# A decoder layer with 64 experts: more expert weights loaded ahead, fewer shared pieces between the experts, wider steps in the last norm

## The chip, the cores and the metric

The kernel runs on one core of a Trainium2 chip. A core has five engines with an instruction queue each: TensorE (PE, matrix products), VectorE (DVE), ScalarE (ACT), GpSimd (POOL) and SyncE (SP, which here only issues transfers). Each works through its own queue in order and waits on semaphores for the others. PE writes to PSUM, from which DVE or ACT must copy a result before its buffer can be written again; all else lies in SBUF or in DRAM. The metric is the device time of one execution in microseconds, lower is better; one number stands for the median of several runs.

## The reference, cut to what matters

The input `x` is 32 batches of 256 tokens of width 256, 8192 tokens in all, in float32. Three sub-layers follow each other, each with a residual and a layer norm after it:

```python
x = _layernorm(x + _L0_attn_ref(x, ...))
x = _layernorm(x + _L0_xattn_ref(x, ctx_1024, ctx_1024, ...))
x = _layernorm(x + _L0_ffn_ref(x, ...))
```

The first two are self-attention with rotary embedding and a differential cross-attention, 16 heads each. The third is a mixture of 64 experts: a router picks 6 experts for each token; each expert takes at most 96 tokens, and computes `gelu(xs @ w1) @ w2` with a hidden width of 128; a token's six results are added with its routing weights. Beside them a shared network of hidden width 512 works on every token:

```python
y = jnp.einsum('ecf,efh->ech', hmid, w2).reshape(E * CAP, h)
out = jnp.zeros((t, h), x.dtype).at[token_of].add(y_pair)
shared = jax.nn.gelu(x @ sw1.T, approximate=True) @ sw2.T
return (out + shared).reshape(b, s, h)
```

## The kernel before, in words

There are two stages, each an `ExitStack` of pools. In the **first stage** (lines 322 to 1141) the 32 batches pass through both attentions. Its end stores, for each batch, the normalised tokens in transposed form in DRAM (`x2T_d`), starts the first accumulator `acc[0]` with them and the second, `acc[1]`, with zeros (`store`, line 1092), and scatters each token's row to the slots of its six experts (`dispatch`, line 1076, POOL's indirect DMAs into `slots`). Small POOL copies (`fence`, line 427) read a `pt` tile in between.

The **shared network** is a generator, `shared` (line 242), over 16 blocks of 512 tokens (`NBLK`). One `next` does one piece: half of a block's first product (8 matmul instructions, into a `two` bank of PSUM, tile `two`), or half of the second product of the block before (16 instructions, into tile `one`). A block is four pieces, 64 in all. The evacuation of a piece on ACT (a GELU into `gT`, or a copy into the block's result `ys[k]`) is kept in `unread` and issued at the next piece by `settle` (line 237). Every fourth piece also issues a load of `x2T` three blocks ahead on SP. Sixteen pieces are issued in the first stage, 48 are left for the second. The results of blocks 0 to 2 have buffers of their own, those of blocks 3 to 15 come from `ypool`.

The **second stage** (lines 1144 to 1367) is a loop over slots. Wrappers named `InOrder` (line 163) hold each engine to the order in which the program issues its instructions. The 64 experts make 32 pairs, `NP`; a pair n passes through four slots from slot n + START on: `turn` (four PE transposes of its rows `xs` into PSUM, copied by DVE to `xsT`), `up` (eight products with `w1`, GELU on ACT to `hT`), `down` (four products with `w2`), and `scatter` (line 1235), in which DVE multiplies by the routing weights into `ye` and POOL issues two indirect DMAs that add the 96 rows of each expert to `acc[0]` and `acc[1]`. The scatter of a pair to one accumulator must wait until that of the pair before has landed. There are six `ye` buffers, eight `xs` buffers, and in PSUM four `one` and two `two` tiles.

The weights of a pair are one tile of 512 KB from the `four` pool, which has ten buffers used in turn (`next_four`, line 1157). `expert_weights` issues the load on SP, `rows_of` the load of the pair's rows. Weights of the first six pairs are issued in slot 1, rows of the first six in slot START - 2, and from then on the rows and weights of pair n + 6 together, after `down(n)` (`fetch_for`, line 1322). A piece of the shared network is issued in each slot below START, and then in two slots out of three until END = START + 35.

From END on, a slot takes a piece, or two in every fourth slot, and one **step of the last norm** (`Last`, line 1258). Block k passes through five parts: `fetch` (SP loads its two accumulators into two `four` tiles, 512 KB each; the first waits for all scatters), `add` (POOL adds them), `stats` (DVE adds the shared result `ys[k]` and takes mean and variance), `scale` (two small ACT instructions, then `rstd` and `off` on POOL), and `put` (four ACT instructions into a third `four` tile, and the output's DMA from ACT's queue). In one step the parts of different blocks are issued in the order of the tuple in lines 1350 to 1356: `fetch` of block s, `add` of s - 1, `scale` of s - 3, `put` of s - 4, `stats` of s - 2. A step whose `stats` needs a shared result that is not yet issued is put off to the next slot (line 1349), while the pieces go on.

Of the kernel before, what the change touches and what calls it, by code (L numbers as in the profile page):

```python
# [12 lines left out]
F32 = mybir.dt.float32  # L13
# [24 lines left out]
def tile_decoder_layer(  # L38
# [194 lines left out]
    NBLK = NT // TB  # L233
    EARLY = min(3, NBLK)
    ys, whole, unread = {}, set(), []
# [86 lines left out]
    with ExitStack() as one:  # L322
# [8 lines left out]
        AHEAD = min(5, B)  # L331
# [812 lines left out]
    with ExitStack() as two:  # L1144

        four = two.enter_context(tc.tile_pool(name="four", bufs=1))
        psum.append(Apart(two))
        wk = two.enter_context(tc.tile_pool(name="wk2", bufs=2))
        small = two.enter_context(tc.tile_pool(name="small2", bufs=3))
        ypool = two.enter_context(tc.tile_pool(name="ypool", bufs=NBLK - EARLY - 1))  # L1150
        ypools.append(ypool)
        AHEAD = 6
        START = 7

        fours = itertools.count()

        def next_four(shape):

            return four.tile(shape, F32, name=f"four{next(fours) % 10}")

        def rows_of(n):

            xs = wk.tile([CAP, 2, XPW], F32, name=f"xs{n % 8}", bufs=1)
            sp.dma_start(
                out=xs,
                in_=slots[2 * n * CAP : (2 * n + 2) * CAP, :].rearrange("(e s) d -> s e d", s=CAP),
            )
            return xs

        def tokens_of(n):  # L1170

            code = xs_of[n][:, :, D + NE]
            empty = small.tile([CAP, 2], F32, tag="empty", name="empty")
            dve.tensor_scalar(empty, code, 0.0, slot_f[:CAP, :], ALU.is_equal, ALU.mult)
            token = small.tile([CAP, 2], F32, tag="token", name="token")
            dve.tensor_scalar(token, code, -1.0, float(NT), ALU.mult, ALU.add)
            idx = small.tile([CAP, 2], I32, name=f"idx{n % 12}", bufs=1)
            dve.tensor_add(idx, token, empty)
            return idx

        def expert_weights(n):

            wt = next_four([P, 2, D // P * F + D])
            sp.dma_start(out=wt, in_=w12[n])
            return wt
# [72 lines left out]
        class Last:  # L1258
# [4 lines left out]
            def fetch(self):  # L1263
                self.sums = []
                for n in range(2):
                    a = next_four([P, NQ, D])
                    sp.dma_start(
                        out=a, in_=acc[n][self.rows, :].rearrange("(p q) d -> p q d", q=NQ)
                    )
                    self.sums.append(a)  # L1270
# [23 lines left out]
            def put(self):  # L1294
                o = next_four([P, NQ, D])
                for q in range(NQ):
                    act.activation(
                        o[:, q, :],
                        ys[self.k][:, q, :],
                        AF.Identity,  # L1300
                        scale=self.rstd[:, q : q + 1],
                        bias=self.off[:, q : q + 1],
                    )
                act.dma_start(
                    out=flat[self.rows, :].rearrange("(p q) d -> p q d", q=NQ), in_=o
                )

        NP = NE // 2
        pairs = [Pair(n) for n in range(NP)]
        xs_of, idx_of, weights_of = {}, {}, {}  # L1310
        last = [Last(k) for k in range(NBLK)]
        END = START + NP + 3
        slot = steps = 0
        more = True

        def pieces_on(n):
            nonlocal more
            for _ in range(n):
                if more:
                    more = next(pieces, "end") != "end"  # L1320

        def fetch_for(n):
            if n < NP:
                xs_of[n] = rows_of(n)
                weights_of[n] = expert_weights(n)

        while more or steps < NBLK + 5:
            n = slot - START

            if 0 <= n - 1 < NP:  # L1330
                pairs[n - 1].turned()
            if 0 <= n - 2 < NP:
                pairs[n - 2].gelu()
            if 0 <= n - 3 < NP:
                pairs[n - 3].scatter()
            if slot == 1:
                for k in range(AHEAD):
                    weights_of[k] = expert_weights(k)
            if slot == START - 2:
                for k in range(AHEAD):  # L1340
                    xs_of[k] = rows_of(k)
            if 0 <= n < NP:
                idx_of[n] = tokens_of(n)

            if slot < START or slot < END and n % 3 < 2:
                pieces_on(1)
            elif slot >= END:
                pieces_on(1 if slot % 4 else 2)
            if slot >= END and (not 2 <= steps < NBLK + 2 or steps - 2 in whole):
                for part, behind in (  # L1350
                    (Last.fetch, 0),
                    (Last.add, 1),
                    (Last.scale, 3),
                    (Last.put, 4),
                    (Last.stats, 2),
                ):
                    if 0 <= steps - behind < NBLK:
                        part(last[steps - behind])
                steps += 1
            if 0 <= n < NP:  # L1360
                pairs[n].turn()
            if 0 <= n - 1 < NP:
                pairs[n - 1].up()
            if 0 <= n - 2 < NP:
                pairs[n - 2].down()
                fetch_for(n - 2 + AHEAD)
            slot += 1


# [60 lines left out]
```

## Time and profile before

| | us |
|---|---|
| median of 6 runs | 1899.2 (1891.34 to 1909.41) |
| the profiled execution's own time | 1895.92 |
| its span in the profile | 1894.2 |
| first piece of the second stage on PE | 1589.6 |
| first turn of a pair on PE | 1627.46 |
| first and last scatter-add issued by POOL | 1636.06, 1812.49 |
| last product of a pair on PE ends | 1786.2 |
| last product of all on PE ends | 1863.9 |
| last output issued by ACT | 1890.54 |

Over the whole span PE is busy for 1803.0 us (95%), ACT 1057.3, DVE 1247.9 and POOL 1192.1; this is the mean of two very different stages, and says little about the second. All instructions carry line 173, that of the helper `InOrder`, so they are told apart by their tiles: `two<-x2T,w_s` and `one<-w_s,gT` are pieces of the shared network, `one<-ident,xs`, `one<-xsT,four` and `one<-four,hT` the turn, up and down of a pair, `acc<-ye,idx` a scatter-add, `four<-in_w` a load of weights, `xs<-slots` of rows, `four<-acc` a fetch of the last norm, `rs`, `rstd` and `off` its scale, `four<-y,off,rstd` its put.

A row of a timeline gives the start, the duration of the run of instructions, the engine (SPq and ACTq are the queues that issue DMAs), line, operation, output and inputs, the count, and in brackets how long the engine was idle before and what released it. A row of the waits gives who waited for whom, total, times and longest. A row of the windows gives, for each engine, its busy time and the number of instructions, then the granted PE clock (1.00 is full), the mean busy share of the 16 DMA engines and the GB/s that they moved.

### The profile page before, as it was taken

The numbers are of one execution on the slowest core, as the hardware profiler recorded it, in microseconds if no ns is written. First come the engines' busy times: TensorE is split into PE (matmuls) and PEld (weight loads), VectorE is DVE, ScalarE is ACT, GpSimd is POOL, SyncE is SP. The second block draws the span as 40 slices with busy tenths as digits, with TensorE's granted clock in tenths as the row PEclk, the third lists the DMA queues.
The fourth block names the chain that finished last, engine by engine and source line by source line (L and its number), as shares of the span: only waits on it lengthen the run. The fifth ranks groups of instructions, "written<-read, shape, count | busy, mean of one in ns | idle before, by whom it ended". The sixth has DMA issues, their size and how long they took to land. (4 is left out here: it accounts for less than half of the span.)

```text
span 1894.2 us, 44636 instructions
## 1 busy us (share of the span) xinstructions
PE 1803.0 (95%) x17800; PEld 1312.4 (69%) x17800; DVE 1247.9 (66%) x2755; ACT 1057.3 (56%) x1807; POOL 1192.1 (63%) x1366
## 2 busy tenths in 40 slices
PE   6999999999999999999999999999999899897973
PEld 4777777777777777777777777777776566575742
DVE  5566677777777777777777777777777452242246
ACT  1666666666666666666666666666666552322237
POOL 7444445777777666777666776666555577244667
PEclk9999999999999999999999999999999899899987
DMA  3080111211111111111111111111112021786478
GB/s 116 15 185 18 32 32 50 70 49 45 39 36 38 35 34 35 35 37 35 36 34 32 33 32 33 33 34 34 32 29 79 18 85 50 233 227 169 81 236 311
DMA packets 109552, 132.16 MB, mean 70 GB/s; under 512 B 33019, under 2 KB 94676, under 8 KB 109344
## 3 DMA queue, kind: packets, MB, share of 16 engines
q1 hardware_dynamic: 78832, 106.83, 18.6%
q0 software_dynamic: 25600, 13.02, 4.1%
q10 hardware_dynamic: 4912, 9.46, 1.3%
q8 instruction: 140, 2.29, 0.5%
q14 instruction: 68, 0.56, 0.1%
HBM read 74.62 MB, written 111.04 MB: 98 GB/s over the span
## 5 line engine op out<-in xcount | busy, mean ns | idle before, releaser
L173 DVE TENSOR_REDUCE pad_mx<-all 128x4 f32<-128x1024 f32 (+1 forms) x512 | 588.9, 1187 | 230.9 <-PE all L173 226.0
L173 ACT ACTIVATE pt<-all 128x512 f32<-128x512 f32 (+3 forms) x768 | 516.6, 740 | 246.2 <-PE all L173 190.0
L173 PE MATMUL all<-qT,kT 32*128 32x256 f32 (+1 forms) x4096 | 517.4, 389 | 3.9 <-DVE qT L173 2.8
L173 PE MATMUL all<-kT,qT 32*128 32x256 f32 (+1 forms) x4096 | 514.6, 386 | 5.6 <-DVE qkb L173 3.0
L173 POOL DMA_INDIRECT slots<-xpt,slot x384 | 387.2, 1008 | 144.3 <-issue 141.6
L173 PEld LDWEIGHTS all<-qT,kT 32*128 32x128 f32 (+1 forms) x4096 | 359.7, 181 | 134.5 <-issue 83.0
L173 PEld LDWEIGHTS all<-kT,qT 32*128 32x128 f32 x4096 | 363.1, 185 | 17.5 <-DVE qkb L173 3.4
L173 POOL TENSOR_TENSOR qT<-qT,mT 128x512 f32<-128x512 f32 x126 | 160.1, 1292 | 135.1 <-ACT mT L173 135.1
L173 PE MATMUL all<-w_qkv,xT 128*128 128x512 f32 (+1 forms) x512 | 183.1, 492 | 8.5 <-DMA xT<-in_xT 8.5
L173 ACT COPY ot<-all 128x512 f32<-128x512 f32 x192 | 112.1, 589 | 94.1 <-PE all L173 90.1
L173 POOL DMA_INDIRECT acc<-ye,idx x64 | 90.2, 1410 | 114.1 <-DVE ye L173 40.6
L173 POOL COPY fence<-pt 120x1 f32<-120x1 f32 (+1 forms) x154 | 28.7, 188 | 165.1 <-ACT pt L173 165.1
L173 PEld LDWEIGHTS all<-w_qkv,xT 128*128 128x128 f32 x512 | 93.7, 193 | 50.7 <-issue 34.8
L173 PE MATMUL all<-pt,pad_xv 120*32 120x256 f32 x2048 | 117.6, 381 | 2.9 <-ACT pt L173 2.8
L173 ACT COPY T<-all 128x512 f32<-128x512 f32 x128 | 73.1, 591 | 80.8 <-PE all L173 77.7
L173 PE MATMUL all<-pt,pad_v 128*32 128x256 f32 x2048 | 117.1, 381 | 0.0
L173 POOL TENSOR_TENSOR rc<-qkb,cosr 128x512 f32<-128x512 f32 x62 | 78.8, 1272 | 51.1 <-DVE qkb L173 50.6
L173 POOL TENSOR_TENSOR pad_qk<-rc,qkb 128x256 f32<-128x256 f32 x124 | 102.5, 848 | 2.7
L173 PE MATMUL all<-ident,ot 128*128 128x128 f32 x768 | 103.4, 278 | 0.1
L173 PE MATMUL two<-x2T,w_s 128*128 128x512 f32 x176 | 84.1, 628 | 19.1 <-ACT gT L173 19.1
L173 PE MATMUL one<-w_s,gT 128*128 128x256 f32 x416 | 95.2, 385 | 5.7 <-DVE ye L173 3.1
L173 PEld LDWEIGHTS all<-ident,ot 128*128 128x128 f32 x768 | 83.6, 141 | 21.5 <-ACT pt L173 13.5
(156 smaller groups left out, 2917.7 us busy)
## 6 DMA issues: line engine op xcount, KB each, us to landing
four<-in_w SPq DMA_DIRECT2D x32, 512.0 KB, 4.5
four<-acc SPq DMA_DIRECT2D x32, 512.0 KB, 6.9
xT<-in_xT SPq DMA_DIRECT2D x32, 256.0 KB, 3.8
xt<-in_x SPq DMA_DIRECT2D x32, 256.0 KB, 4.1
x2T_d<-T SPq DMA_DIRECT2D x32, 256.0 KB, 2.5
acc<-xpt SPq DMA_DIRECT2D x32, 256.0 KB, 2.7
acc<-zero SPq DMA_DIRECT2D x32, 256.0 KB, 3.4
x2T<-x2T_d SPq DMA_DIRECT2D x16, 512.0 KB, 6.9
```

Source lines behind the costliest of these rows:

```text
L173: ins = f(*args, **kwargs)
```

## The change

The pool `four` gets 14 buffers in place of 10, and `ypool` 8 in place of 12, so the room is the same. The weights of 14 pairs are issued in slot 1, and after `down(n)` the rows of pair n + 6 and the weights of pair n + 14. The first pair starts in slot 6 in place of 7. While pairs pass, a shared piece is issued in one slot of three in place of two. In the last norm `add`, `stats`, `scale` and `put` follow `fetch` by 2, 3, 5 and 6 steps in place of 1, 2, 3 and 4; a step is put off when its `stats`, now three steps behind, lacks its shared result.

```diff
-        ypool = two.enter_context(tc.tile_pool(name="ypool", bufs=NBLK - EARLY - 1))
+        ypool = two.enter_context(tc.tile_pool(name="ypool", bufs=8))
...
         AHEAD = 6
-        START = 7
+        FOURS = 14
+        START = 6
...
-            return four.tile(shape, F32, name=f"four{next(fours) % 10}")
+            return four.tile(shape, F32, name=f"four{next(fours) % FOURS}")
...
-        def fetch_for(n):
-            if n < NP:
-                xs_of[n] = rows_of(n)
-                weights_of[n] = expert_weights(n)
-
-        while more or steps < NBLK + 5:
+        def fetch_after(n):
+
+            if n + AHEAD < NP:
+                xs_of[n + AHEAD] = rows_of(n + AHEAD)
+            if n + FOURS < NP:
+                weights_of[n + FOURS] = expert_weights(n + FOURS)
+
+        while more or steps < NBLK + 7:
...
-                for k in range(AHEAD):
+                for k in range(FOURS):
                     weights_of[k] = expert_weights(k)
...
-            if slot < START or slot < END and n % 3 < 2:
+            if slot < START or slot < END and n % 3 == 0:
                 pieces_on(1)
             elif slot >= END:
                 pieces_on(1 if slot % 4 else 2)
-            if slot >= END and (not 2 <= steps < NBLK + 2 or steps - 2 in whole):
+            if slot >= END and (not 3 <= steps < NBLK + 3 or steps - 3 in whole):
                 for part, behind in (
                     (Last.fetch, 0),
-                    (Last.add, 1),
-                    (Last.scale, 3),
-                    (Last.put, 4),
-                    (Last.stats, 2),
+                    (Last.add, 2),
+                    (Last.scale, 5),
+                    (Last.put, 6),
+                    (Last.stats, 3),
                 ):
...
-                fetch_for(n - 2 + AHEAD)
+                fetch_after(n - 2)
```

## The prediction

> **What bounds the kernel now.** The change touches only the second stage, from 1589.6 us on; everything before it stays as it is. I read the waits first, then the stage in windows, then the engines one by one in the timeline. What TensorE (PE) waited for in this stage:
>
> ```profile
> engine line waited for: us in total, times, longest us
> PE two L173 <- ACT gT L173: 19.1, 2, 12.0
> PE one L173 <- DVE ye L173: 10.7, 5, 3.7
> ```
>
> No weight tile stands among PE's releasers: PE never waited for an expert's weights. It waited twice for a GELU on ScalarE (ACT), 7.1 us at 1610 and 12.0 us at 1817, and for `ye` in between. The timeline of GpSimd (POOL) says why: the scatter-adds into `acc` form two chains, one for each accumulator, in which each waits until the one before has landed.
>
> ```profile
> 1702.30 1.41 POOL L173 DMA_INDIRECT acc<-ye,idx  x1 [4.75 <-DVE ye L173]
> 1704.01 1.41 POOL L173 DMA_INDIRECT acc<-ye,idx  x1 [0.30 <-issue]
> 1708.52 1.41 POOL L173 DMA_INDIRECT acc<-ye,idx  x1 [3.11 <-DVE ye L173]
> ...
> 1798.74 1.41 POOL L173 DMA_INDIRECT acc<-ye,idx  x1 [0.97 <-DMA acc<-ye,idx]
> 1800.45 1.41 POOL L173 DMA_INDIRECT acc<-ye,idx  x1 [0.30 <-issue]
> 1802.85 1.41 POOL L173 DMA_INDIRECT acc<-ye,idx  x1 [0.99 <-DMA acc<-ye,idx]
> ```
>
> A pair takes 6.22 us at 1702 and 4.11 us at 1799. The windows show what differs:
>
> ```profile
> core 0: us, PE busy (x) PEld busy (x) DVE busy (x) ACT busy (x) POOL busy (x), PEclk, DMA share, GB/s
> 1637.86:1760.23 122.37, 111.28 (x589) 84.57 (x588) 41.59 (x141) 26.40 (x40) 53.53 (x39) 0.97 0.77 202
> 1760.23:1812.49 52.26, 52.26 (x226) 36.80 (x226) 10.60 (x35) 14.22 (x16) 33.80 (x24) 1.00 0.45 55
> ```
>
> While SyncE's (SP) queue moves weights and rows (DMA share 0.77), 19 pairs take 122.37 us, 6.44 each; after the last load at 1754 (share 0.45), 12 pairs take 52.26 us, 4.36 each. `ye` has six buffers, so PE runs six pairs ahead and then stands still with the chain. I call S the issue of the last scatter, 1812.5. Everything later hangs on it: the last norm's first fetch waits for the scatters.
>
> **The sum, part by part.** Unit costs from PE's timeline: a shared piece (`two<-x2T,w_s` or `one<-w_s,gT`) takes 3.43 us (two start at 1786.20, the next at 1793.07); turn, up and down of a pair take 2.09 us (1696.21 to 1698.30).
>
> *Weights earlier.* They cannot start earlier than now:
>
> ```profile
> 1605.70 0.20 POOL L173 COPY fence<-pt 120x1 f32<-120x1 f32 x1
> 1605.93 2.81 SPq L173 DMA_DIRECT2D four<-in_w  x6
> ```
>
> SP waited 33.0 us for that POOL instruction. So 14 loads leave at 1605.93 and not 6, ahead of the `x2T` load and of the rows `xs` on the same queue. At the 400 GB/s of the windows 1608 to 1616 one load of 512 KB moves in 1.31 us: 14 x 1.31 = 18.3, `x2T` 1.31, the first rows 0.87 (240.8 KB at 285 GB/s, windows 1616 to 1624), and some 2.2 us until they land (3.1 median less 0.87): 1628.7. The first turn is at 1627.46 now, with one piece after it; with START = 6 that piece goes, but PE comes out of a pause and finds the next rows 0.87 us apart. I take the first scatter 1 us earlier (1635); bounds 3 us earlier, 3 later.
>
> Later each slot issues rows for n+6 as before and weights for n+14. These go into the buffer that `down(n)` has just read, so SP now waits for PE; behind it are the next slot's rows, needed four slots later, and `x2T`, needed twelve pieces later: nothing.
>
> *The scatter chain.* Its excess now is 19 x (6.44 - 4.36) = 39.6 us. SP moved 24 rows (20.9 us), 24 weights (31.4) and 5 `x2T` (6.6) in that time, 58.9 us: 0.67 us of delay for each us of transfer. After: 25 rows (21.8), 18 weights (23.6), 3 `x2T` (3.9), 49.3 us, so 33.0 of excess: **6.6 us gained**. Bounds: nothing gained, if the delay comes with the rows, which stay; 39.6 if it vanished wholly. Proportion is nearest to the rows I have. S becomes 1812.5 - 6.6 - 1 = 1804.9.
>
> *One piece in three slots.* 48 pieces remain at the stage's start, both times. Before, 31 are done by the end of the pairs (7 + 24); after, 18 (6 + 12). PE work per pair falls from 4.4 to 3.2 us, beside a chain of 4.4 to 6.4 us which PE only follows: nothing gained there. But **30 pieces instead of 17, 13 x 3.43 = 44.6 us, move behind the pairs**. Part fills PE's time while the scatters drain. Now the last `down` ends at 1786.2, S - 26.3, and that lead stays.
>
> One rule stands against these emptier slots. After a pause of 2.28 us at 1713 four `down` matmuls took 1.65 us, not 1.03, and the piece after them 4.80, not 3.60. The Trainium skill (TensorE: Matmul & The Clock Gate, What's actually happening) says that PE falls to half rate after an idle window of about 3.4 us. By it a pieceless slot would cost 4.2 us of PE and three slots 15.3, which is 2.2 over three unloaded periods, some 9 us for the last 12 pairs. The sum takes nothing for it. By the row a pause costs 0.6 + 1.2 = 1.8 us of PE; a loaded pair leaves PE 3.2 us idle and an unloaded one 1.1, with six pairs of lead to draw on. Bounds: 0, and 12 x (1.8 - 1.1) = 8.4 us.
>
> *Steps further apart.* ACT works in order, and its `scale(0)` waits for the first fetch, its sum and its statistics. Evacuations behind it wait too, so PE stops when PSUM is full. Now and then:
>
> ```profile
> 1813.75 3.60 PE L173 MATMUL two<-x2T,w_s 128*128 128x512 f32 x8
> 1829.32 6.51 PE L173 MATMUL two<-x2T,w_s 128*128 128x512 f32 x8 [11.98 <-ACT gT L173]
> 1835.67 7.07 PE L173 MATMUL one<-w_s,gT 128*128 128x256 f32 x32
> ```
>
> PE resumes at S + 16.8, and its first piece takes 2.9 us more than usual. After, `scale(0)` stands in the sixth slot of the end. Seven pieces are issued by then, with six evacuations ahead of it on ACT; the next ones fill two `two` and four `one` buffers, so PE does 12 pieces, 41.2 us, up to S + 14.9. The 13th needs a `two` whose GELU stands on ACT behind `put(0)`; that waits for `rstd(0)`, and on POOL `add(3)` comes before it, where `add(2)` did:
>
> ```profile
> 1827.27 3.24 POOL L173 TENSOR_TENSOR four<-four,four 128x1024 f32<-128x1024 f32 x1 [0.23 <-DMA four<-acc]
> 1830.47 1.05 POOL L173 TENSOR_TENSOR rstd<-rs,mhalf 128x4 f32<-128x4 f32 x1
> 1831.59 0.24 POOL L173 TENSOR_TENSOR off<-off,rstd 128x4 f32<-128x4 f32 x1
> ```
>
> Adds started at 1821.15, 1824.70 and 1827.27, so a fourth some 10 us after the first, S + 18.5, ends at S + 20.9; `rstd` and `off` take 1.4 (S + 22.3), `put(0)` 2.08 and its DMA issue 0.38, an evacuation 0.49, the GELU 1.8, handovers 0.6: **PE resumes at S + 27.6**. It has 18 pieces left, 61.7 us, and the slow start of 2.9: PE ends at **S + 92.2** (now S + 51.4).
>
> The steps cost ACT 2.77 us each (0.29 + 2.10 + 0.38, start to start) and POOL 3.63. In a slot, 1.25 pieces cost ACT 1.4 and PE 4.3, so PE leads by little. The fetches, outputs and late `x2T` loads, some 27 MB at 390 GB/s, 69 us from S + 5, end earlier. The 14 buffers let seven blocks come at once; that brings nothing while PE ends last.
>
> *Tail.* Step 18 waits for the last piece. Behind it on ACT: an evacuation 0.49, three `scale` 0.87, four `put` 8.4, three DMA issues 1.14, and 3.7 from the last issue to the span's end (1890.5 to 1894.2): 14.6. End: 1804.9 + 92.2 + 14.6 = **1911.7, 17.5 us longer** than the span of 1894.2. The profiled execution's own time is 1895.9, so 1913.4; the median shown, 1899.2, is 3.3 above that execution, so **1916.7**.
>
> *Smaller `ypool`.* Block 11 reuses block 3's buffer; its writer and the reader that frees it are both on ACT, `put(3)` ahead of it in program order. No wait. It costs only if an evacuation came first; it does not.
>
> **Rivals.** *Weights alone delay the scatters* (for it: they move the most; against: rows go with every one of the 19 slow pairs). Then from pair 11 on, PE being six ahead at weight 17, the chain runs at 4.36: excess 11 x 2.08 = 22.9, 16.7 gained, 10.1 more than forecast: +7.4, **1906.6**. *The chain runs free* and ends on the other side: loads seven pairs further ahead no longer meet the scatters, S = 1812.5 - 39.6 - 1 = 1771.9, end 1878.7, -15.5, **1883.7**. It decides against me from S = 1777.9 (1884.7 - 106.8) down; 18 weights and 25 rows still flowing speak against it. *ACT ends last, or PE is cold*: ACT's 4.2 us a slot against PE's 4.3 leaves no room; half a us more in each of some 18 slots, or the 8.4 us above, adds 9 and gives +26.5, **1925.7**. *The change does nothing* is true of its weights (no wait for them exists); the pieces move all the same, so I give it nothing of its own.
>
> **How the numbers follow.** Forecast 0.62, around 1916.7, with its own range 1909 to 1923; weights alone 0.18; ACT or cold PE 0.13; free chain 0.07. What a measurement of this kernel tells from no change is about 0.5%, 9.5 us. Weights alone falls within it; the forecast's range begins above. Slower 0.75, same 0.18, faster 0.07. The range leaves out the free chain and the ends beyond: 1900 to 1929.
>
> **What would show it.** Right: first weights still near 1606, first rows near 1628; the last scatter near 1805, slow pairs up to about the 12th to 19th; a PE pause of 10 us or more after the last scatter; PE busy until some 15 us before the end, with four `put` behind it. Wrong: S below 1780; PE pausing little after S; PE done 25 us or more before the end, as now.

## The result and the profile after

The changed kernel takes 1912.72 us (median of 20 runs, 1909.95 to 1919.30), the kernel before 1901.26 us (46 runs, 1889.40 to 1912.06): the ratio is **1.0069 [1.0055, 1.0084]**, slower by about 0.7%. (The ratio with its 95% interval is not quite the quotient of the two medians, which is 1.0060.) The profiled execution took 1915.67 us, with a span of 1914.0.

The second stage is read in three parts, for every kernel of this study: the **start**, from the POOL `fence` copy that releases SP (1605.70 before, 1607.82 after) to the first scatter; the **chain**, from the first scatter to the issue of the last, S; and the **end**, from S to the end of the span. Counting from the fence takes out what the first stage does: over all the executions below except two on a chip of their own, the end of the first stage scatters by 6.7 us without a change in its code. These are the windows of the kernel before, cut at these points (columns as in the prediction's windows):

```profile
1605.70:1636.06 30.36, 23.25 (x94) 15.89 (x93) 4.08 (x17) 10.57 (x11) 3.13 (x5) 0.83 0.76 238
1636.06:1812.49 176.43, 165.34 (x821) 122.93 (x821) 52.19 (x175) 40.62 (x56) 88.83 (x63) 0.98 0.67 158
1812.49:1894.20 81.71, 39.22 (x135) 26.16 (x133) 53.03 (x144) 51.15 (x109) 60.25 (x49) 0.76 0.84 311
```

And of the changed kernel:

```profile
1607.82:1641.47 33.65, 20.88 (x75) 14.99 (x74) 3.99 (x17) 8.03 (x9) 3.13 (x5) 0.80 0.84 286
1641.47:1804.23 162.76, 140.49 (x708) 104.89 (x707) 51.96 (x175) 30.97 (x47) 88.78 (x63) 0.94 0.66 144
1804.23:1914.00 109.77, 80.01 (x275) 52.65 (x273) 64.94 (x144) 63.45 (x120) 71.03 (x49) 0.87 0.63 250
```

Start +3.3, chain -13.7, end +28.1: together +17.7 us. PE's busy time says what moved: 24.9 us less in the chain, 40.8 us more after it. Before, the end ran at 311 GB/s with PE busy for 39 of 82 us; after, PE is busy for 80 of 110.

The waits of PE in the second stage, to be held against the table that the prediction opens with:

```profile
engine line waited for: us in total, times, longest us
PE one L173 <- DVE ye L173: 20.4, 9, 4.3
PE two L173 <- ACT rs L173: 13.6, 1, 13.6
PE one L173 <- DMA xs<-slots: 7.2, 1, 7.2
PE two L173 <- ACT gT L173: 6.9, 3, 5.5
```

The wait for `ye` has doubled: PE has less of its own to do and stands longer at the chain. The pause behind the last scatter is still there (12.0, now 13.6, put down to `rs`). One wait is new: 7.2 us for the first rows, `xs`.

**The start** on SP's queue and on PE (a run of DMA issues, then two runs of matmuls):

```profile
1608.05 10.94 SPq L173 DMA_DIRECT2D four<-in_w  x14
...
1621.28 7.92 SPq L173 DMA_DIRECT2D xs<-slots  x7
```

```profile
1632.34 1.62 PE L173 MATMUL one<-ident,xs 96*128 96x96 f32 x8 [7.23 <-DMA xs<-slots]
1634.03 2.00 PE L173 MATMUL one<-xsT,four 128*128 128x96 f32 x8
```

Fourteen loads now stand ahead of the rows. PE waits for them until 24.5 us after the fence, and is then slow: eight products with `w1` take 2.00 us, where in the start of the kernel before they took 1.06.

**The chain** in two windows, from the second scatter of pair 0 to that of pair 12, and on to S:

```profile
1643.27:1716.98 73.71, 60.58 (x349) 48.02 (x347) 28.96 (x99) 12.85 (x24) 33.80 (x24) 0.93 0.86 223
1716.98:1804.23 87.25, 78.11 (x355) 56.15 (x356) 23.00 (x77) 18.12 (x23) 53.48 (x38) 0.94 0.49 73
```

Twelve pairs at 6.14 us, then nineteen at 4.59; the last weights are issued at 1713.30, near the end of the first window, the last rows at 1746.87. Before, nineteen pairs were slow. PE pauses in this time, and after some of its pauses it is slow:

```profile
1702.52 6.57 PE L173 MATMUL one<-w_s,gT 128*128 128x256 f32 x16 [4.32 <-DVE ye L173]
...
1730.92 1.10 PE L173 MATMUL one<-four,hT 128*96 128x256 f32 x4 [1.99 <-DVE ye L173]
1731.87 5.29 PE L173 MATMUL two<-x2T,w_s 128*128 128x512 f32 x8
...
1761.33 3.72 PE L173 MATMUL one<-w_s,gT 128*128 128x256 f32 x16 [3.06 <-DVE ye L173]
```

**The end** on PE, around the pause, and the last put with its DMA issue on ACT:

```profile
1776.19 1.03 PE L173 MATMUL one<-four,hT 128*96 128x256 f32 x4
1777.05 7.03 PE L173 MATMUL two<-x2T,w_s 128*128 128x512 f32 x16
...
1811.46 7.07 PE L173 MATMUL one<-w_s,gT 128*128 128x256 f32 x32
1832.14 10.04 PE L173 MATMUL two<-x2T,w_s 128*128 128x512 f32 x16 [13.60 <-ACT rs L173]
...
1885.32 13.98 PE L173 MATMUL one<-w_s,gT 128*128 128x256 f32 x64
```

```profile
1908.19 2.07 ACT L173 ACTIVATE four<-y,off,rstd 128x256 f32<-128x256 f32 x4 [0.42 <-ACT four L173]
1910.30 0.34 ACTq L173 DMA_DIRECT2D out<-four  x1
```

The last `down` ends at 1777.2, 27.0 us ahead of S. Twelve pieces (six at each tile) follow to 1818.5, S + 14.3; PE resumes at S + 27.9 and ends at 1899.3, S + 95.1, 14.7 us before the span's end. Before, PE's last run was this one:

```profile
1857.91 6.31 PE L173 MATMUL one<-w_s,gT 128*128 128x256 f32 x28 [0.54 <-ACT rs L173]
```

It ended at 1864.2, S + 51.7 (the 1863.9 in the table ahead of the prediction is 0.3 us too early), and 30.0 us of norm and output followed it.

### The profile page after: what moved, and what is told of

The parts are those of the page before. It is cut to its first block, busy times and chain, and to the rows that moved or that the text cites. A ratio compares the mean times of both kernels' runs of the same rounds, so it can differ in the third digit from the quotient of the medians.

```text
span 1914.0 us, 44632 instructions
## 1 busy us (share of the span) xinstructions
PE 1818.5 (95%) x17800; PEld 1320.5 (69%) x17800; DVE 1259.3 (66%) x2755; ACT 1057.0 (55%) x1807; POOL 1201.1 (63%) x1366
## 4 chain that ended last, share of the span: by engine, by line
PE 77%; DMA 8%; POOL 7%; issue 4%; ACT 2%; DVE 2%; SPq 0%; POOLq 0%; ACTq 0%; DVEq 0%
PE all L173 74%; DMA acc<-ye,idx 6%; POOL slots L173 3%; PE one L173 2%; POOL rstd L173 1%; POOL four L173 1%; PE two L173 1%; DVE ye L173 1%; ACT four L173 1%; DMA four<-in_w 1%; ACT pt L173 1%; DMA xs<-slots 1%; DMA four<-acc 0%; POOL qT L173 0%; ACT gT L173 0%
## 5 line engine op out<-in xcount | busy, mean ns | idle before, releaser
L173 PEld LDWEIGHTS all<-kT,qT 32*128 32x128 f32 x4096 | 363.3, 185 | 17.5 <-DVE qkb L173 3.3
L173 POOL COPY fence<-pt 120x1 f32<-120x1 f32 (+1 forms) x154 | 28.4, 186 | 167.5 <-ACT pt L173 165.8
L173 PE MATMUL two<-x2T,w_s 128*128 128x512 f32 x176 | 84.6, 633 | 20.5 <-ACT rs L173 13.6
L173 PEld LDWEIGHTS one<-w_s,gT 128*128 128x128 f32 x416 | 83.2, 201 | 27.0 <-DVE ye L173 8.2
```

The source lines that it names most:

```text
L173: ins = f(*args, **kwargs)
```

## The experiments

All times are in us and from one profile each; ratios, with their 95% intervals, are to the kernel before on the same chip. Loads in the chain are counted on SP's queue between first and last scatter: W weights (1.31 us each by the prediction), R rows (0.87), X `x2T` (1.31).

| kernel | start | chain | end | fence to end | ratio to before [95%] |
|---|---|---|---|---|---|
| before | 30.4 | 176.4 | 81.7 | 288.5 | 1 |
| before, second profile (c1) | 30.6 | 179.9 | 82.1 | 292.6 | |
| changed | 33.7 | 162.8 | 109.8 | 306.2 | 1.0069 [1.0055, 1.0084] |
| e1 six ahead | 24.6 | 170.9 | 110.6 | 306.1 | 1.0059 [1.0041, 1.0077] |
| e2 steps close | 32.9 | 162.8 | 109.7 | 305.4 | 1.0069 [1.0051, 1.0088] |
| e3 twelve ahead, two in three | 33.6 | 170.2 | 80.6 | 284.5 | 0.9944 [0.9923, 0.9966] |
| e4 without late weights | 32.6 | 145.9 | 110.2 | 288.7 | |
| e5 e3 with rows first | 27.0 | 167.1 | 80.8 | 274.9 | 0.9918 [0.9891, 0.9945] |
| e6 changed, rows first | 24.6 | 167.5 | 111.2 | 303.3 | 1.0061 [1.0037, 1.0085] |
| e7 without late rows | 32.6 | 150.3 | 111.1 | 294.0 | |
| e8 before with START = 6 | 25.4 | 177.5 | 81.9 | 284.9 | 0.9931 [0.9907, 0.9956] |
| e9 as e5 | 25.6 | 168.0 | 80.6 | 274.1 | 0.9920 [0.9905, 0.9934] |
| e10 as e8 | 27.3 | 173.0 | 81.1 | 281.4 | 0.9947 [0.9918, 0.9976] |
| e11 as e5 | 26.6 | 165.4 | 81.4 | 273.4 | 0.9906 [0.9875, 0.9937] |

The theory: the 13 pieces moved behind the pairs lengthen the end, and the weights sent earlier shorten the chain by a part of their transfer. The rivals: the wider steps make the end longer; the burst of 14 loads, which holds back the first rows, is the cost; the weights alone, and not the rows, delay the scatters.

**e1: the changed kernel with weights six ahead again.**

```diff
-                for k in range(FOURS):
+                for k in range(AHEAD):
...
-            if n + FOURS < NP:
-                weights_of[n + FOURS] = expert_weights(n + FOURS)
+            if n + AHEAD < NP:
+                weights_of[n + AHEAD] = expert_weights(n + AHEAD)
```

> The changed kernel with the weights of six pairs ahead again (slot 1 loads six, later n + 6); pieces, steps, buffers stay as changed. Theory A (the 13 pieces moved behind the pairs make PE end last; earlier weights shorten the scatter chain): the first scatter comes some 5 us earlier (1636), the chain is as long as before or nearly (170 to 176 us in place of 162.8), the last scatter (S) at 1806 to 1812, PE ends some 95 us after it as in the changed kernel, time 1914 to 1921. Rival B (the burst of 14 loads, which holds back the first rows, is the cost): the time falls to 1905 or less. Rival C (the wider steps of the norm are the cost): as A, 1914 or more.

Measured: 1912.71, against 1912.72 for the changed kernel: a little less than the theory expected, and far above the 1905 at most of the rival that the burst is the cost. Its first and last scatter:

```profile
1627.04 1.50 POOL L173 DMA_INDIRECT acc<-ye,idx  x1 [20.71 <-ACT gT L173]
...
1797.95 1.41 POOL L173 DMA_INDIRECT acc<-ye,idx  x1 [1.01 <-DMA acc<-ye,idx]
```

With six loads ahead of the rows the first scatter goes out 24.6 us after the fence, with fourteen 33.7: the burst costs 9.0 us. It then saves 8.1 us of the chain (162.8 against 170.9; W 24, the first of them 0.06 us ahead of the first scatter, R 23, X 2 here; W 17, R 24, X 2 in the changed kernel). **Eight more weights ahead bring nothing in this order of the queue**: what the chain gains, the start has paid.

**e2: the changed kernel with the old steps of the last norm.**

```diff
-                    (Last.add, 2),
-                    (Last.scale, 5),
-                    (Last.put, 6),
-                    (Last.stats, 3),
+                    (Last.add, 1),
+                    (Last.scale, 3),
+                    (Last.put, 4),
+                    (Last.stats, 2),
```

> The changed kernel with the steps of the norm as they were (add 1, stats 2, scale 3, put 4 behind). Theory A: S unchanged (1804); PE does some 10 pieces before it stops, resumes at S + 17 in place of S + 28, has 20 left, ends at S + 88 to S + 90, and three puts in place of four follow: 6 to 9 us less than the changed kernel, 1903 to 1907, still not faster than before. Rival C (wider steps are the whole cost): 1900 or less. Rival B: no difference, 1911 to 1914.

Measured: the same ratio, 1.0069, and an end of 109.7 us. PE after the last `down`:

```profile
1794.92 7.07 PE L173 MATMUL one<-w_s,gT 128*128 128x256 f32 x32
1817.87 5.21 PE L173 MATMUL two<-x2T,w_s 128*128 128x512 f32 x8 [15.88 <-ACT gT L173]
1825.18 3.70 PE L173 MATMUL two<-x2T,w_s 128*128 128x512 f32 x8 [2.11 <-ACT rs L173]
...
1883.81 13.98 PE L173 MATMUL one<-w_s,gT 128*128 128x256 f32 x64
```

The gain of 6 to 9 us expected of it did not come. PE resumes 11 us earlier, at S + 16.9, as before the change; but only 8 pieces were done by then, not the 10 expected or the 12 of the changed kernel, so 22 are left and PE ends at S + 96.8 (changed: S + 95.1). Wider steps let PE do more pieces ahead of its pause, and make the pause end later by as much. The steps are neutral.

**e3: two pieces in three slots again, old steps, room shared 12 and 10.** Besides e2's edit:

```diff
-        ypool = two.enter_context(tc.tile_pool(name="ypool", bufs=8))
+        ypool = two.enter_context(tc.tile_pool(name="ypool", bufs=10))
...
-        FOURS = 14
+        FOURS = 12
...
-            if slot < START or slot < END and n % 3 == 0:
+            if slot < START or slot < END and n % 3 < 2:
```

> The changed kernel with a piece in two slots of three again and the steps as they were, the room divided into 12 weight tiles and 10 block results (12 pairs ahead). Theory A: 17 pieces are left behind the pairs, PE ends some 30 us before the end again, the end is at S + 82; with 20 loads of weights beside the chain S is 1805 to 1811: 1889 to 1895 in the span, a time of 1892 to 1899, at or below before. Rival B (the burst of loads): 1905 or more. Rival C (steps): about 1900 too, so C is told from A by the run with the steps alone.

Measured: 1890.54, ratio 0.9944 [0.9923, 0.9966]: **on the other side of the kernel before**, with the same weights policy but for two buffers. The end is 80.6 us long, 29.2 shorter than in the changed kernel, PE ends 24 us before the span does, and the chain is 7.5 us longer. Its last scatter and its last run on PE:

```profile
1807.68 1.41 POOL L173 DMA_INDIRECT acc<-ye,idx  x1 [0.95 <-DMA acc<-ye,idx]
```

```profile
1857.77 6.31 PE L173 MATMUL one<-w_s,gT 128*128 128x256 f32 x28 [0.43 <-ACT rs L173]
```

By medians on one chip e3 takes 24.3 us less than e2, from which it differs in the pieces and in the two buffers. With the steps neutral (e2), and the end as long with six weights ahead as with fourteen (e1), the pieces are the cost of the change. No run changes the size of `ypool` alone; but in the changed kernel's end ACT's waits before it writes a block's result `y` are for PE (11.5 us in all) and for its own `put` (1.3 us), so the smaller pool can have held it up by little.

**e4 and e7: what a transfer costs the chain.** In the changed kernel, the weights after the first 14 are not loaded (e4), or the rows after the first six (e7):

```diff
-                weights_of[n + FOURS] = expert_weights(n + FOURS)
+                weights_of[n + FOURS] = weights_of[n + FOURS - 8]
```

> The changed kernel without the loads of the weights of the last 18 pairs, which use tiles loaded for others instead, so that part of the computation is left out. It measures what the loads cost the scatter chain. In proportion to transfer time (0.67 us per us, 18 x 1.31): S 16 us earlier, at 1788, and the end 16 us earlier too, since all hangs on S. If weights alone delay the scatters: the chain at 4.4 us a pair from the start, 139 us, S at 1780. If the rows do it: S stays at 1804.

```diff
-                xs_of[n + AHEAD] = rows_of(n + AHEAD)
+                xs_of[n + AHEAD] = xs_of[n % AHEAD]
```

> The changed kernel without the loads of the rows of pairs 6 to 31, which work on the first six pairs' rows instead, so that part of the computation is left out. With the run without the late weights (18 loads, 24 us of transfer, shortened the chain by 16.9 us) it tells what delays the scatters. If every transfer counts alike: 25 row loads, 22 us of transfer, shorten the chain by some 15 us, to 147 or 148. If weights alone delay them: 160 or more. If rows, issued as the scatters leave, count more: 140 or less.

The windows of the two chains, e4 first:

```profile
1641.68:1787.61 145.93, 132.86 (x704) 100.85 (x703) 51.92 (x175) 31.01 (x47) 88.84 (x64) 0.96 0.55 91
```

```profile
1635.03:1785.28 150.25, 134.54 (x704) 101.69 (x703) 51.63 (x175) 31.00 (x47) 88.82 (x64) 0.95 0.58 114
```

Without the 18 weights that the changed kernel issues from 1640 on (23.6 us of transfer) the chain is 16.8 us shorter than the changed kernel's, 0.71 us for each us; without the 25 row loads from 1640 on (21.8 us; one more, issued with the first six, is left out too) it is 12.5 us shorter, 0.57 for each us. Each stands on one profile, and the chain of one kernel scatters by 3.5 us (below), so 0.71 and 0.57 are not told apart. Neither kind is alone at fault: the rival that the weights alone delay the scatters falls, and so does one that only the rows do. Counting all loads alike gave 0.67 in the prediction, between the two.

**The kernel before, profiled again**, to see how far its parts scatter.

> The kernel before once more, for a second profile. The last POOL fence of the first stage came at 1605.7 in the profile of before and at 1607.8, 1602.4, 1605.3, 1603.8 and 1609.1 in those of five kernels with the same first stage; the second stage is measured from it. If the first stage's end is all that scatters, the stretch from that fence to the end is 288.5 us again (286 to 291). If the second stage of before scatters too, it is longer here, and the 17.7 us by which the changed kernel's stretch was longer (306.2) shrink towards the 11 to 13 us of the medians.

The start repeats to 0.3 us and the end to 0.4, the chain only to 3.5 us (e8 and e10 further down, one kernel on two chips, differ by 4.5). So the second stage scatters too: its 292.6 us lie outside the 286 to 291 of the first case. Differences of chains below some 4.5 us between two single profiles are not read here.

**e5: e3 with the rows ahead of the weights beyond the sixth.** Slot 1 loads six weights, and the other six follow the rows in slot START - 2:

```diff
             if slot == 1:
-                for k in range(FOURS):
+                for k in range(AHEAD):
                     weights_of[k] = expert_weights(k)
             if slot == START - 2:
...
+                for k in range(AHEAD, FOURS):
+                    weights_of[k] = expert_weights(k)
```

> The kernel with 12 weight tiles, 10 block results, a piece in two slots of three and the old steps (1890.5), with the first rows issued ahead of weights 6 to 11: slot 1 loads six pairs' weights, then come the rows of six pairs, then the other six weights. Theory (the burst costs at the start what it saves in the chain): the first scatter comes 25 to 28 us after the last fence in place of 33.6, the chain stays at 170 to 173 us, S and the end come 5 to 8 us earlier: 1882 to 1886. Rival (the six late weights collide with the first scatters, or PE is the limit at the start): S as before, 1889 to 1892.

Measured: 1883.39, ratio 0.9918 [0.9891, 0.9945]. SP's queue in its start:

```profile
1607.38 3.02 SPq L173 DMA_DIRECT2D four<-in_w  x6
...
1616.38 2.80 SPq L173 DMA_DIRECT2D xs<-slots  x6
1619.22 5.11 SPq L173 DMA_DIRECT2D four<-in_w  x6
```

The start is 27.0 us, 6.6 shorter than with twelve weights in front, and in this profile the chain did not give that back (167.1 against 170.2).

**e6: the same order of the queue in the changed kernel**, with its 14 weights, one piece in three and wide steps.

> The changed kernel with its first rows issued ahead of weights 6 to 13, nothing else. Theory (burst of 14 costs 9 us at the start, earlier weights save 8 us of chain): first scatter 25 to 28 us after the last fence in place of 33.7, chain 163 to 167 us, S 5 to 8 us earlier, PE's end and the whole 5 to 8 us earlier: 1905 to 1908, still slower than before because the 13 pieces stay behind the pairs. Rival (start and chain trade against each other whatever the order): 1911 to 1914.

Measured: 1910.78, ratio 1.0061 [1.0037, 1.0085], hardly less than the 1.0069 of the changed kernel: the expectation was too hopeful, and its rival, that start and chain trade against each other, is nearer. The start shrank by 9.0 us, but the chain grew by 4.7: its first four pairs took 35.5 us (27.9 in the changed kernel), as the eight weights now pass beside them. And PE, which ends last here, still has its 30 pieces behind the pairs.

**e8 and e10: the kernel before with START = 6 and nothing else**, against **e9 and e11: e5 again.** What does a first pair that is one slot earlier bring by itself? On the chip of e8 and e9 everything took longer from the first stage on (before: 1942.71); only ratios and parts are read there.

```diff
-        START = 7
+        START = 6
```

> The kernel before with START = 6 in place of 7, nothing else: six pairs' weights ahead, ten tiles, twelve block results, a piece in two slots of three. It is the fast variant (12 tiles, rows first) without its earlier weights. If earlier weights are worth what the changed kernel's chain showed (8 us of chain), this kernel's chain stays at 174 to 180 us with the first scatter 25 to 27 us after the last fence: 4 to 6 us faster than before, 6 to 10 us slower than the fast variant. If the earlier start is the whole gain: as fast as the fast variant, within 3 us.

> The fast variant once more (12 tiles, 10 block results, two slots of three, old steps, rows ahead of weights 6 to 11), beside the one above on the same chip: 0.992 of the kernel before again (0.989 to 0.995), chain 167 us, stretch from the last fence to the end 275 us.

> The kernel before with START = 6 once more. In the first comparison the profiles set it 10 us behind the fast variant (stretch from the last fence to the end 284.9 against 274.1), the medians only 1.8 us (ratios 0.9931 and 0.9920). If earlier weights (12 ahead, rows first) are worth the profile's 10 us, the ratios are again apart, by 0.003 or more, in the fast variant's favour, and the chain here is 174 to 180 us. If they are worth nothing, the ratios agree within 0.002 and this profile's chain is nearer to 170.

> The fast variant (12 tiles, 10 block results, two slots of three, old steps, rows ahead of weights 6 to 11) on the same chip as the one above: 0.992 of the kernel before, chain 167 us, stretch from the last fence to the end 275 us, whichever holds.

START = 6 alone gave 0.9931 and 0.9947, and e5's kernel 0.9918, 0.9920 and 0.9906 in its three trials. **Both beat the kernel before, and e5's is the fastest seen, 0.8 to 0.9% ahead of the kernel before.** More than half of that is START = 6, which takes one piece away ahead of the first turn; 4 to 6 us were expected of it, and by medians it brought 13.7 and 11.9, more than the profiles show from fence to end (3.6 to 11.2 against the two of before), and why is open. So the change contains a step that is a gain by itself, and its 11.5 us of loss understate what the moved pieces cost; e3, which has START = 6 and twelve weights in front, is no faster than START = 6 alone. Earlier weights behind the rows take off another 0.001 to 0.004 of the time by the ratios (some 2 to 8 us), 1.8 and 5.1 us by the medians on the two chips, and 8 to 11 us from fence to end by profiles (273.4 against 281.4, 274.1 against 284.9); the intervals overlap, so their size is not settled.

## Why the prediction was right, and where its sum was off

The direction and the size held: 1916.7 was forecast and 1912.72 measured, inside the forecast's own range of 1909 to 1923. As a ratio to its own base it said 1916.7 / 1899.2 = 1.0092, somewhat above the measured 1.0055 to 1.0084: it forecast 17.5 us more, and the medians differ by 11.5. Step by step:

- **The first weights cannot start earlier: right.** SP issues 0.23 us after the fence, as before.
- **First rows and first scatter: wrong, a mis-sized term.** The rows were forecast 23.0 us after the fence (1628.7 - 1605.7), and PE got them after 24.5. The first scatter was to come 1 us earlier; counted from the fence it came 3.3 us later, just beyond the bound of 3 later. The forecast let one piece less in front of the first turn (START = 6) pay for the later rows; the runs show that the burst costs 9.0 us (e1), and that PE, having stood 7.23 us, did the first pair at half its speed (2.00 for 1.06, 1.91 for 1.03).
- **The chain: right in kind, mis-sized.** It was to lose 6.6 us and lost 13.7 (17.2 against the second profile of before). One cause can be named. The loads beside it fell more than was counted: before W 24, R 23, X 6, 59.3 us; after W 17, R 24, X 2, 45.8; 13.5 us of transfer and not 9.6. At the forecast's 0.67 that makes 9.0 us. What is left is 4.7 us, near the scatter of single profiles, and was not taken apart. From e1 to the changed kernel 8.3 us less of transfer went with 8.1 us less of chain, about 1 us for each us; but 3.5 us of scatter leave room for 0.67 there, and e4 and e7 gave 0.71 and 0.57. That S was forecast at 1804.9 and came at 1804.23 is luck: the chain was shorter by 7.1 us than forecast, the start longer by 4.3, and the first stage ended 2.1 us later.
- **13 pieces behind the pairs: right, and the cause of the result.** Counted by slots 13 moved; one of them stood in the slot after the last `down` before the change as well, so behind the last `down` PE has 30 pieces where it had 18, 41.2 us more. PE's end moved from S + 51.7 to S + 95.1, 43.4 us; beside the pieces stand a pause that is 1.6 us longer and 0.9 us of further waits, against a last `down` somewhat further ahead of S. The forecast's 92.2 less its 51.4 was 40.8. The span's end moved by 28.1, because before 30.0 us followed PE and now 14.7. e3 gives the end back.
- **The pause: right in every place.** Last `down` at S - 27.0 (forecast S - 26.3), twelve pieces to S + 14.3 (S + 14.9), resumed at S + 27.9 (S + 27.6), PE's end S + 95.1 (S + 92.2). The missing 2.9 us are a resumption 0.3 us later, two more waits for a GELU of 0.7 each and a remainder of 1.1. That the steps caused the later resumption was right too, but it was no cost: with the old steps PE resumes earlier and has more left (e2). Had the forecast worked out the old steps with 30 pieces, it would have seen that.
- **The tail: right.** After the last piece ACT has an evacuation, three `scale`, four `put`: 14.7 us for 14.6.
- **The clock gate, for which the sum took nothing: right in the result.** PE's pauses in the chain did make it slow: after 4.32 us of standing a piece took 6.57 us, after 3.11 us eight products took 1.97 and not 1.06, and after only 1.99 us, with one `down` between, a piece took 5.29; after 3.06 us another piece took only 3.72. The granted clock was 0.55 from 1702.52 to 1708.90, 0.71 from 1730.92 to 1736.90 and 1.00 from 1761.33 to 1764.80; over the chain it fell from 0.98 to 0.94. But the last `down` stayed 27.0 us ahead of S, so PE's lead paid for it. The Trainium skill (TensorE: Matmul & The Clock Gate, What's actually happening), with its idle window of about 3.4 us, agrees in kind; the slow work after 1.99 and 3.11 us, like the row at 1713 in the kernel before, lies below that figure, so the length of the pause just before does not tell here whether PE is slow after it.
- **The rivals.** The free chain needed S below 1777.9, and S was 1804.23. "Weights alone" falls by e4 and e7. ACT did not end last: PE's last run ends 14.7 us before the span, with the four `put` behind it that were forecast.

The profiles differ by 17.7 us from fence to end (15.7 against the mean of the two profiles of before), the medians by 11.5. Of the two profiled executions that of before lies 5.3 us under its median and that of the changed kernel 3.0 us over, so 8.3 of the 19.8 us between their spans come from which executions were profiled. In which parts these lie is open: the chain of one and the same kernel scatters by 3.5 us between profiles, and the first stage ends 6.7 us apart, which may hide part of it but was not followed up.

## What to carry to other kernels

A filler that uses an engine's idle time beside a chain of another engine is worth its whole length only until the chain ends: before moving it, work out what the engine has left at that moment and which engine then ends last. A prefetch that stands in the same queue ahead of the first data that is needed delays that data by most of its transfer: here eight loads, some 10.5 us at the prediction's 1.31 us each, held the first scatter back by 9.0 us. The same loads a few places later cost nothing there (24.6 us, e6), though the first pairs then ran beside them, and with the old pieces that order was the faster one by 0.002 to 0.004, with intervals that overlap. When an order of steps lengthens a pause, count what was done ahead of the pause before calling it a cost.

## What the runs showed of the hardware that was not expected

In the changed kernel DVE's sum `y<-y,four` takes 2.30 us, where it takes 1.23 with the old steps, and POOL's small `rstd` 2.00 and not 1.02 (medians). The instructions by tile, with shortest/median/longest in ns, of the changed kernel and then of e2:

```profile
L173 POOL TENSOR_TENSOR rstd<-rs,mhalf x16: 1006/2000/2027, 1824.8 to 1905.8; 128x4 f32<-128x4 f32 x16
L173 DVE TENSOR_TENSOR y<-y,four x16: 1224/2297/3347, 1815.4 to 1900.0; 128x1024 f32<-128x1024 f32 x16
```

```profile
L173 POOL TENSOR_TENSOR rstd<-rs,mhalf x16: 1007/1020/2012, 1819.3 to 1902.5; 128x4 f32<-128x4 f32 x16
L173 DVE TENSOR_TENSOR y<-y,four x16: 1224/1226/2348, 1812.1 to 1898.6; 128x1024 f32<-128x1024 f32 x16
```

The timelines of POOL and DVE in the changed kernel show that the two meet:

```profile
1831.60 2.36 POOL L173 TENSOR_TENSOR four<-four,four 128x1024 f32<-128x1024 f32 x1
1833.92 2.00 POOL L173 TENSOR_TENSOR rstd<-rs,mhalf 128x4 f32<-128x4 f32 x1
```

```profile
1832.74 2.30 DVE L173 TENSOR_TENSOR y<-y,four 128x1024 f32<-128x1024 f32 x1
```

DVE's sum starts 1.14 us into POOL's `add` and ends 1.08 us after it, little less than it takes by itself; `rstd` starts with the `add`'s end and ends 0.88 us after DVE's sum. Each seems to stand until the other is through. The Trainium skill (SBUF — State Buffer, SBUF: two separate sides) describes that: a GpSimd instruction and a VectorE instruction with two SBUF inputs share a pair of ports, and the one that starts first keeps it for its whole length. The rows agree with it; no run here takes the two apart to show it. It is not quite without a price: the first `rstd`, on which `put(0)` and so the end of PE's pause hangs, takes 2.03 us at 1824.81, where the forecast had 1.05. That is 1 us of a pause which came out 0.3 us later than forecast; and e2, where the two hardly meet, is as long.
